# Image 0 of a four-image vision kernel: rows scanned first, and its preparation chained chunk by chunk into the scan

## The chip, the core and the metric

The kernel runs as one program on one core of a Trainium2 chip. The metric is the device time of that core in microseconds (us), from a launch to the last output written. Before the change the median of three runs was 8837.66 us (8813.62 to 8846.13).

## What is computed

The input is a batch of four images, `x` of 4 x 96 x 64 x 64 floats. Three layers follow one another on each image, and the images do not depend on each other.

```python
# layer 0: a selective scan in four directions (k = 0..3), Di = 192 channels, N = 16 states
u      = silu(depthwise_conv3x3(in_proj(norm(x))))
z      = silu(in_proj_z(norm(x)))
delta  = softplus(dt_w[k] @ x_proj[k](u) + dt_b[k])
h      = exp(delta * A) * h + (delta * u) * B          # one step per pixel, 4096 pixels
y_k    = sum_n(h * C) + D * u                          # k=0 rows, 1 columns, 2 and 3 the same backwards
x1     = x + out_proj(norm(y_0 + y_1 + y_2 + y_3) * z)
# layer 1: a deformable 3x3 convolution: offsets from a convolution, then gathers from a table of pixels
# layers 2 and 3: a Fourier mixer, a quantised MLP, a linear attention, a quantised MLP
```

Direction 0 reads an image by rows and direction 2 the same backwards; 1 and 3 read it by columns.

## The kernel before, in words

A Python program writes the instructions of all engines, and keeps its own model of when each engine will be free (`Clock`, line 207). What it writes down is the order on each engine; the chip then runs each engine's list in that order. Three strands are woven together.

The **scan** (`Layer0.scan`, line 816) is the spine. It works through 1536 units: 4 images x 4 directions x 4 steps of 1024 pixels x 24 groups of 8 channels. A unit loads its decays (`fetch`, line 882, on ScalarE's DMA queue), takes their exponential (line 932, ScalarE), spreads its inflow over the states with a matmul (line 938, TensorE), multiplies it with B (line 952, VectorE), runs the recurrence (line 960, VectorE), multiplies with C (line 969, GpSimd) and is summed into a total (line 988, TensorE). The inputs of a unit are fetched from DRAM: B and C once per step (`fetch_step`, line 913), the inflow `du` once per eight units (`fetch_block`, line 920), both on SyncE's queue. Before image 0's first unit is written, `scan` asks for the chunks it needs (`made`, line 835: a chunk is 512 pixels, a step is two chunks). While they are missing it lets the other strands run alone.

The strand **`ends`** (line 1721) prepares images and finishes them: `before(0)`, the constants of layers 2 and 3, `before(1)` to `before(3)`, and then layers 2 and 3 of images 0 to 3, one after the other (`Layers23.image`, line 1688, which first waits until layer 1 of its image is over). The strand **`middle`** (line 1731) writes zeros into the border of the two gather tables (`Layer1.cleared`, line 1125), and then does, image by image, the end of layer 0 (`behind`, line 1010) and layer 1 (`Layer1.image`, line 1139: offsets, positions, and `sample`, line 1284, with one gather per pixel and tap). Beside each unit of the scan the program puts pieces of these two strands where its model finds room. When the scan is over, both strands run to their end.

`before(b)` (line 592) prepares an image in stages, each of which is over before the next begins. `inputs` (615) loads `x`; `normed_rows` (635) normalises it into a padded tile `pad`; `convolved` (672) then loads its weights `wc` and `wz`, and makes the depthwise convolution and the gate `z` for 8 chunks, 18 + 2 matmuls and six loads of an activation table to a chunk, with the results `xa` and `xc` stored to DRAM. After that `before` loads the weights of the projections, and for each chunk makes `projected` (729, both orientations, q = 1 and 0) and six chains of `steps` (751): directions 1, 0+1, 3, 2+3, 0, 2. A chain with two directions holds the last 64 channels of both. A chain is a matmul `pd`, a softplus on ScalarE, VectorE and GpSimd, the store of `de` (delta) to DRAM, a product with u, its split into three bf16 parts by matmuls `pr` and copies, and the store of `du`.

`pipe` (line 273) runs a few such chains side by side: up to `width`, of which a later one may take no step that the earlier ones have not taken `every` + 1 steps before, with three PSUM banks and counted tiles (`ex`, `lw`, `rl`, `du`, `zt`).

SyncE's queue takes its DMAs in order. Where one DMA has to wait for another, or for an engine, all that stand behind it wait as well. Of the eight border writes four go to each table, and they overlap at the corners, so that each waits until the one before it on its table has landed.

Of the kernel before, what the change touches and what calls it, by code (L numbers as in the profile page):

```python
# [272 lines left out]
def pipe(net, chains, width, every=0, **tiles):  # L273
# [5 lines left out]
    while True:  # L279
        if more and len(active) < width:  # L280
            steps = next(chains, None)
            if steps is None:
                more = False
            else:
                active.append(Chain(steps, clock.now()))
                continue
        if not active:
            break
        for n, chain in enumerate(active):
            if chain.new and not net.has_bank():  # L290
                continue
            if any(a.done <= chain.done + every for a in active[:n]):
                continue
            if not all(free[tag] > 0 for tag in chain.takes):
                continue
            if clock.has_room(known.get((chain.kind, chain.done), (1.0,) * 4), chain.ready):
                break
        else:
            yield BLOCKED
            continue  # L300
        for tag in chain.takes:
            free[tag] -= 1
        clock.precede(known.get((chain.kind, chain.done), (0.0,) * 4))
        step = next(chain.steps, None)
        if step is None:
            net.hold(-chain.holds)
            active.remove(chain)
            end = max(end, chain.ready)
            continue
        for tag in step.frees:  # L310
            free[tag] += 1
        known[chain.kind, chain.done] = step.work
        chain.ready = clock.queue(step, chain.ready)
        chain.done += 1
        net.hold(step.holds - chain.holds)
        chain.holds, chain.new, chain.takes = step.holds, step.new, step.takes
        yield None
# [221 lines left out]
class Layer0:  # L539
# [51 lines left out]

    def before(self, b):
        net = self.net
        tc, nc, ins = net.tc, net.nc, net.ins
        with tc.tile_pool(name=f"l0u{b}", bufs=1) as up:
# [3 lines left out]
            with tc.tile_pool(name=f"l0b{b}", bufs=1) as sm:  # L599
# [5 lines left out]
                def chains():  # L605
                    yield self.projected(b, 0, us, xp_a, xp_c, sm, xdbl)
                    for j in range(NCH):
                        for ks in ((1,), (0, 1), (3,), (2, 3), (0,), (2,)):
                            yield self.steps(b, ks, j, us, dtw, sm, xdbl)
                        if j + 1 < NCH:  # L610
                            yield self.projected(b, j + 1, us, xp_a, xp_c, sm, xdbl)
# [3 lines left out]
    def inputs(self, b, up, us):  # L615

        tc, nc, ins = self.net.tc, self.net.nc, self.net.ins
# [4 lines left out]
        nc.sync.dma_start(x, ins["x"][b])  # L622

        def rows(pad, j):
            return pad[:, 1 + j * NR : 1 + (j + 1) * NR, 1 : 1 + W]

        def as_rows(t):
            return t.rearrange("p (h w) -> p h w", w=W)

        with tc.tile_pool(name=f"l0a{b}", bufs=1) as big:  # L630
            pad = big.tile([C, PW, PW], F32, name=f"pad{b}", tag="pad")
            yield from self.normed_rows(b, x, pad, rows, as_rows)
            yield from self.convolved(b, pad, xa, xc, rows, as_rows)

    def normed_rows(self, b, x, pad, rows, as_rows):

        net = self.net
# [34 lines left out]
    def convolved(self, b, pad, xa, xc, rows, as_rows):  # L672

        net = self.net
        tc, nc, ins = net.tc, net.nc, net.ins
        with tc.tile_pool(name=f"l0i{b}", bufs=1) as sm:
            wc = sm.tile([C, 9, 256], F32, name=f"wc{b}", tag="wc")
            nc.sync.dma_start(wc, self.wc_d)
            wz = sm.tile([C, 256], F32, name=f"wz{b}", tag="wz")
            nc.sync.dma_start(wz, ins["w_in"][:, 256:])  # L680
            yield wait(4.0)
            xct_v = xc.rearrange("p (w h) -> p h w", h=H)

            def chain(j):
                cs = slice(j * CH, (j + 1) * CH)
                r0 = j * NR
                for g in range(2):
                    pp = net.mm(f"pc{g}_{b}_{j}")
                    for q in range(9):
                        dy, dx = divmod(q, 3)  # L690
                        nc.tensor.matmul(  # L691
                            pp,
                            lhsT=wc[:, q, g * 128 : (g + 1) * 128],
                            rhs=pad[:, r0 + dy : r0 + dy + NR, dx : dx + W],
                            start=(q == 0),
                            stop=(q == 8),
                        )
                        if q < 8:
                            yield cost(pe=0.8, holds=1)
                    if g == 0:  # L700
                        nc.scalar.activation(xa[:, cs], pp, AF.Silu, bias=net.vec(V_CBA))
                    else:
                        nc.scalar.activation(xc[:64, cs], pp[:64], AF.Silu, bias=net.vec(V_CBC, 64))
                        nc.scalar.activation(
                            xct_v[64:, r0 : r0 + NR, :],
                            as_rows(pp[64:]),
                            AF.Silu,
                            bias=net.vec(V_CBC, 64, 64),
                        )
                    net.exp_and_log()  # L710
                    yield cost(pe=0.8, act=4.0, new=True, takes="zt" if g else "")
                zts = []
                for g, (c0, n) in enumerate(((0, 128), (128, D2))):
                    pz = net.mm(f"pz{g}_{b}_{j}")
                    nc.tensor.matmul(pz, lhsT=wz[:, c0 : c0 + 128], rhs=rows(pad, j), start=True, stop=True)
                    zt = sm.tile([128, CH], F32, name=f"zt{g}_{b}_{j}", tag=f"zt{g}")
                    nc.scalar.activation(zt[:n], pz[:n], AF.Silu)
                    zts.append((c0, n, zt))
                net.exp_and_log()
                yield cost(pe=2.0, act=3.8)  # L720
                for c0, n, zt in zts:
                    nc.sync.dma_start(self.z_d[b][c0 : c0 + n, cs], zt[:n])
                nc.sync.dma_start(self.u_d[b][:128, cs], xa[:, cs])
                nc.sync.dma_start(self.u_d[b][128:, cs], xc[:64, cs])
                yield wait(frees="zt")

            yield from pipe(self.net, (chain(j) for j in range(NCH)), 2, zt=1)

    def projected(self, b, j, us, xp_a, xp_c, sm, xdbl):
# [5 lines left out]
        for q in (1, 0):  # L735
# [9 lines left out]
            yield cost(pe=1.3, act=0.7, new=q == 1)  # L745
        for q in (1, 0):
# [4 lines left out]
    def steps(self, b, ks, j, us, dtw, sm, xdbl):  # L751
# [14 lines left out]
        for k in ks:  # L766
            q = k % 2
            o, m = (pd[64 * q : 64 * q + 64], slice(128, DI)) if both else (pd, slice(0, 128))
            nc.tensor.matmul(o, lhsT=dtw[:, k, m], rhs=xdbl[q, j], start=True, stop=True)  # L769
# [14 lines left out]
        if not both and ks[0] % 2:  # L784
# [31 lines left out]
    def scan(self):  # L816
# [5 lines left out]
            for k in (1, 3, 0, 2)  # L822
# [889 lines left out]
def layers23(net, x2, out):  # L1712
# [4 lines left out]
    with ExitStack() as ctx:  # L1717
# [3 lines left out]
        def ends():  # L1721
            yield from l0.before(0)
# [8 lines left out]
        def middle():  # L1731
            yield from l1.cleared()
# [59 lines left out]
```

## Time and profile before

| What | us |
|---|---|
| median of three runs | 8837.66 |
| the profiled execution's own time | 8879.74 |
| its span, first to last instruction | 8877.9 |
| first recurrence (line 960) starts | 359.4 |
| last recurrence starts | 7667.6 |
| last gather of layer 1 (line 1301) starts | 8350.2 |
| VectorE busy (share of the span) | 6807.1 (77%) |
| TensorE busy | 6652.4 (75%) |
| GpSimd busy | 5620.9 (63%) |
| ScalarE busy | 4943.6 (56%) |

The profiled execution took 42 us more than the median of the runs. The span falls into a head without scan (to 359 us), the scan (to 7670 us) and a tail in which the two strands run out (to 8878 us). Shares of the whole span hide this: what bounds the time has to be read in each of the three.

In the lines shown below a piece of the chain of waits has its start in us, its length in us, and its engine or DMA with the tile written and the tile read; a letter and number such as L691 is a line of the kernel. A row of the table by stretches has the limits in us, and for each engine its busy time with the number of instructions in brackets, then the granted TensorE clock as a share of full speed, the DMA engines' busy share and GB/s.

### The profile page before, as it was taken

Reading aid. Unit: us, or ns where it says so; the run is one execution under the profiler, and the core shown is the slowest. Engines: PE = TensorE matmul, PEld = TensorE weight load, DVE = VectorE, ACT = ScalarE, POOL = GpSimd, SP = SyncE. Lnnn points to the kernel's source line nnn. Section 1 sums busy time; section 2 is a strip of 40 time slices with the busy share of each in tenths; the row PEclk is TensorE's granted clock in tenths of the full one; section 3 lists DMA queues with packets and bytes.
Section 4 is the critical chain, followed back from the end, with each engine's and each line's share of the span. In section 5 each row is a group of like instructions: output and inputs, shape, how many; then the busy total and the mean of one; then the engine's idle time right before and its main releaser. Section 6 shows DMA issues by size and latency. Waiting matters only on the chain.

```text
span 8877.9 us, 96298 instructions
## 1 busy us (share of the span) xinstructions
PE 6652.4 (75%) x31960; PEld 2922.8 (33%) x31960; DVE 6807.1 (77%) x5091; ACT 4943.6 (56%) x9062; POOL 5620.9 (63%) x4307
## 2 busy tenths in 40 slices
PE   6665967687767778777667888776778877787797
PEld 2111311122122224311222455222445532265383
DVE  0488889987888988788898887788878888636514
ACT  3564656555556768745566666445656774423323
POOL 0365656665668888666588888566887886447400
PEclk8786977788778779877777888787888887788797
DMA  1476777767678888876788988676888987444310
GB/s 48 134 201 178 187 186 223 202 176 184 190 204 228 234 225 231 212 181 187 200 226 223 230 223 225 152 181 173 212 228 211 234 204 170 108 128 146 96 55 11
DMA packets 775989, 1608.40 MB, mean 181 GB/s; under 512 B 247809, under 2 KB 339357, under 8 KB 773382
## 3 DMA queue, kind: packets, MB, share of 16 engines
q10 hardware_dynamic: 244224, 843.17, 37.0%
q1 hardware_dynamic: 457542, 532.51, 22.2%
q0 software_dynamic: 73728, 226.57, 9.7%
q8 instruction: 256, 4.19, 0.2%
q14 instruction: 239, 1.96, 0.1%
HBM read 1345.62 MB, written 256.29 MB: 180 GB/s over the span
## 4 chain that ended last, share of the span: by engine, by line
PE 35%; DVE 28%; DMA 16%; ACT 8%; issue 8%; POOL 3%; SPq 2%; ACTq 1%; DVEq 0%; another core or an unknown queue 0%; POOLq 0%
DVE hh L960 14%; DVE db L952 7%; DMA du<-du 6%; PE pc L691 4%; PE py L988 4%; PE f L1428 3%; PE db L938 3%; PE ps L1334 3%; DMA da<-de 2%; ACT g L1313 2%; PE pd L1350 2%; POOL hh L969 1%; ACT da L932 1%; PE h L1469 1%; PE py L983 1%
## 5 line engine op out<-in xcount | busy, mean ns | idle before, releaser
L969 POOL TENSOR_TENSOR hh<-hh,bc 128x1024 f32<-128x1024 f32 x1536 | 3659.8, 2385 | 346.0 <-DVE hh L960 233.6
L960 DVE TENSOR_TENSOR_SCAN hh<-da,st,db 128x1024 f32<-128x1024 f32 x1152 | 2701.0, 2345 | 236.2 <-PE py L988 98.9
L952 DVE TENSOR_TENSOR db<-db,bc 128x1024 f32<-128x1024 f32 x1536 | 1863.3, 1213 | 557.5 <-PE db L938 551.6
L932 ACT ACTIVATE da<-da,w_al 128x1024 f32<-128x1024 f32 x1536 | 1741.8, 1146 | 648.2 <-DMA da<-de 295.3
L938 PE MATMUL db<-du,rep 96*128 96x512 bf16 x3072 | 1105.0, 448 | 810.8 <-DVE hh L960 748.9
L1301 POOL DMA_INDIRECT g<-table,idx x1152 | 1210.6, 1051 | 407.2 <-issue 176.0
L988 PE MATMUL py<-hh,w_fold 128*32 128x512 f32 x6144 | 1055.6, 762 | 26.6 <-POOL hh L969 8.8
L1313 ACT ACTIVATE g<-g,wt 128x96 f32<-128x96 f32 x3456 | 963.9, 364 | 167.6 <-DMA du<-du 52.2
L960 DVE TENSOR_TENSOR_SCAN hh<-da,db 128x1024 f32<-128x1024 f32 x384 | 877.1, 2284 | 68.9 <-PE py L988 22.8
L938 PEld LDWEIGHTS <-rep 96*128 96x128 bf16 x3072 | 284.5, 107 | 1764.0 <-issue 1126.3
L1334 PE MATMUL ps<-w_ident,g 128*96 128x128 f32 x3744 | 675.3, 320 | 215.0 <-ACT g L1313 138.0
L780 POOL TENSOR_TENSOR lw<-lw,w 128x512 f32<-128x512 f32 x192 | 244.2, 1272 | 825.5 <-DVE w L778 815.6
L967 POOL COPY st<-hh 128x1 f32<-128x1 f32 x1152 | 232.4, 202 | 725.3 <-DVE hh L960 682.0
L1334 PEld LDWEIGHTS ps<-w_ident,g 128*96 128x96 f32 x3744 | 480.1, 141 | 569.4 <-ACT g L1313 249.6
L691 PE MATMUL pc<-pad,wc 96*128 96x512 f32 x1152 | 547.8, 615 | 53.4 <-DMA wc<-wc_d 46.3
L1342 ACT COPY st<-ps 96x384 f32<-96x384 f32 x384 | 179.7, 472 | 458.2 <-PE ps L1334 350.6
L801 PE MATMUL pr<-ex,w_ident 128*128 128x512 f32 x384 | 281.0, 822 | 170.0 <-DVE ex L791 87.7
L778 DVE SCALAR_TENSOR_TENSOR w<-w,ex 128x512 f32<-128x512 f32 x192 | 155.1, 808 | 289.8 <-ACT w L775 289.7
L691 PEld LDWEIGHTS pc<-pad,wc 96*128 96x128 f32 x1152 | 216.5, 195 | 336.4 <-issue 305.1
L988 PEld LDWEIGHTS py<-hh,w_fold 128*32 128x32 f32 x6144 | 155.1, 123 | 516.8 <-issue 393.8
L769 PE MATMUL pd<-xd,w_dtw 103*64 103x512 f32 (+1 forms) x512 | 268.0, 802 | 65.8 <-DVE rl L782 26.1
L1350 PE MATMUL pd<-st,wdc 96*128 96x256 f32 x1152 | 302.4, 411 | 7.8 <-ACT st L1342 4.1
(250 smaller groups left out, 8807.7 us busy)
## 6 DMA issues: line engine op xcount, KB each, us to landing
da<-de ACTq DMA_DIRECT2D x1536, 512.0 KB
du<-du SPq DMA_DIRECT2D x512, 192.0 KB
bc<-bcd SPq DMA_DIRECT2D x128, 512.0 KB
du<-du SPq DMA_DIRECT2D x128, 384.0 KB
y<-yb SPq DMA_DIRECT2D x384, 128.0 KB
de<-rl SPq DMA_DIRECT2D x128, 256.0 KB
m<-in_dft SPq DMA_DIRECT2D x128, 256.0 KB
ad<-y ACTq DMA_DIRECT2D x192, 128.0 KB
```

Source lines behind the costliest of these rows:

```text
L691: nc.tensor.matmul(pp, lhsT=wc[:, q, g * 128 : (g + 1) * 128], rhs=pad[:, r0 + dy : r0 + dy + NR, dx : dx + W], start=(q == 0), stop=(q == 8),
L801: nc.tensor.matmul(pr, lhsT=net.ident, rhs=ex, start=True, stop=False)
L932: self.net.nc.scalar.activation(u.da, u.da, AF.Exp, scale=self.al[:, a : a + 1])
L938: self.net.nc.tensor.matmul(db[:, h, :], lhsT=self.rep[:96, u.s % 4, :], rhs=u.du[u.s // 4][:, h * CH : (h + 1) * CH], start=True, stop=True,)
L952: self.net.nc.vector.tensor_mul(u.db, u.db, u.bc[:, 0, :])
L960: nc.vector.tensor_tensor_scan(u.along(u.hh), u.along(u.da), u.along(u.db), first, ALU.mult, ALU.add)
L969: self.net.nc.gpsimd.tensor_mul(u.hh, u.hh, u.bc[:, 1, :])
L988: nc.tensor.matmul(py[p0 : p0 + 32], lhsT=self.fold[:, u.i, :], rhs=hc[:, h * CH : (h + 1) * CH], start=u.sums["add"] is None and u.i == 0 ...
L1301: nc.gpsimd.indirect_dma_start(out=g[:, k, :], out_offset=None, in_=self.tables[b % 2], in_offset=bass.IndirectOffsetOnAxis(ap=idx[:, n : ...
L1313: nc.scalar.activation(pixel, pixel, AF.Identity, scale=wt[:, n, c : c + 1])
L1334: nc.tensor.matmul(pt[:, k, :], lhsT=g[:, k, c * C : (c + 1) * C], rhs=net.ident, is_transpose=True, start=(c == 0), stop=(c == corners - 1),)
L1350: nc.tensor.matmul(po, lhsT=wdc[:, k, :], rhs=st[:, k, :], start=(k == 0), stop=(k == 8))
```

## The change

Image 0 gets a preparation of its own, `first`, in the place of `before(0)`:

- `wc`, `wz` and the weights of the projections are requested right behind `x`, before the normalisation.
- The convolution of chunk j+1, the row projection of chunk j and its three chains of `steps` (directions 0, 0+2, 2) are now in one `pipe` of width 6; the projection of chunk j waits for a token that the convolution of chunk j gives. The `lane` argument lets convolutions be ordered among themselves only, and the other chains among themselves only. The columns (1, 1+3, 3) follow in a second `pipe`.
- The scan of image 0 takes the directions in the order 0, 1, 3, 2 instead of 1, 3, 0, 2.
- A chain 0+2 or 1+3 holds two directions of one orientation. Its product with u, one instruction before, is two instructions of 64 partitions, one of which reads a turned view.
- `middle` waits for the first recurrence before it clears the borders.

Images 1 to 3 are prepared as before.

```diff
-def pipe(net, chains, width, every=0, **tiles):
+def pipe(net, chains, width, every=0, lane=None, **tiles):
...
-            if any(a.done <= chain.done + every for a in active[:n]):
+            if any(
+                a.done <= chain.done + every
+                for a in active[:n]
+                if lane is None or (a.kind is lane) == (chain.kind is lane)
+            ):
                 continue
...
+    def first(self):
...
+        with tc.tile_pool(name=f"l0u{b}", bufs=1) as up, tc.tile_pool(name=f"l0b{b}", bufs=1) as sm:
+            us = []
+            x = self.tokens(b, up, us)
+            xp_a, xp_c = (net.load(q, sm) for q in ("xp_a", "xp_c"))
+            dtw = net.load("dtw", sm)
+            xdbl = {}
+            with tc.tile_pool(name=f"l0a{b}", bufs=1) as big, tc.tile_pool(name=f"l0i{b}", bufs=1) as cp:
+                pad = big.tile([C, PW, PW], F32, name=f"pad{b}", tag="pad")
+                weights = self.conv_weights(b, cp)
+                yield from self.normed_rows(b, x, pad)
+
+                def rows_first():
+                    yield self.conv(b, 0, pad, us, weights, cp)
+                    for j in range(NCH):
+                        if j + 1 < NCH:
+                            yield self.conv(b, j + 1, pad, us, weights, cp)
+                        yield self.projected(b, j, us, xp_a, xp_c, sm, xdbl, (0,), f"c{j}")
+                        for ks in ((0,), (0, 2), (2,)):
+                            yield self.steps(b, ks, j, us, dtw, sm, xdbl)
+
+                tokens = {f"c{j}": 0 for j in range(NCH)}
+                yield from pipe(
+                    net, rows_first(), 6, every=2, lane=Layer0.conv.__code__,
+                    ex=3, lw=1, rl=2, du=2, zt=1, **tokens,
+                )
+
+            def columns():
+                for j in range(NCH):
+                    yield self.projected(b, j, us, xp_a, xp_c, sm, xdbl, (1,))
+                    for ks in ((1,), (1, 3), (3,)):
+                        yield self.steps(b, ks, j, us, dtw, sm, xdbl)
+
+            yield from pipe(net, columns(), 5, every=2, ex=3, lw=1, rl=2, du=2)
...
+    def conv_weights(self, b, sm):
+
+        nc = self.net.nc
+        wc = sm.tile([C, 9, 256], F32, name=f"wc{b}", tag="wc")
+        nc.sync.dma_start(wc, self.wc_d)
+        wz = sm.tile([C, 256], F32, name=f"wz{b}", tag="wz")
+        nc.sync.dma_start(wz, self.net.ins["w_in"][:, 256:])
+        return wc, wz
+
+    def conv(self, b, j, pad, us, weights, sm):
...
-                yield wait(frees="zt")
+        yield wait(frees=f"zt c{j}")
...
+        if both and ks[0] % 2 == ks[1] % 2:
+            q, xc = ks[0] % 2, us[2]
+            own, far = slice(64 * q, 64 * q + 64), slice(64 - 64 * q, 128 - 64 * q)
+            turned = xc.rearrange("p (a b) -> p b a", a=64)
+            nc.vector.tensor_mul(ex[own], rl[own], xc[own, cs])
+            nc.vector.tensor_mul(
+                ex[far].rearrange("p (a b) -> p a b", b=64),
+                rl[far].rearrange("p (a b) -> p a b", b=64),
+                turned[far, j * NR : (j + 1) * NR, :],
+            )
...
-            for k in (1, 3, 0, 2)
+            for k in ((1, 3, 0, 2) if b else (0, 1, 3, 2))
...
-            yield from l0.before(0)
+            yield from l0.first()
...
         def middle():
+            while not l0.scanned[1]:
+                yield BLOCKED
             yield from l1.cleared()
```

The body of `conv` is that of the chain in `convolved`, moved into a method of its own.

## The prediction, on record before the changed kernel ran

> **What bounds the kernel now.** I read the table by stretches first, because the shares of the whole span mix three different stages.
>
> ```profile
> 0.00:357.00 357.00, 215.83 (x450) 84.24 (x451) 38.94 (x69) 155.83 (x193) 14.83 (x19) 0.81 0.23 67
> 357.00:7670.00 7313.00, 5489.00 (x24594) 2183.59 (x24594) 6243.02 (x4241) 4441.81 (x8179) 5229.06 (x3975) 0.80 0.78 202
> 7670.00:8414.00 744.00, 570.52 (x3888) 389.67 (x3888) 397.99 (x565) 208.74 (x420) 373.20 (x312) 0.79 0.42 120
> 8414.00:8878.00 464.00, 377.06 (x3028) 265.33 (x3028) 127.16 (x217) 137.18 (x270) 3.83 (x1) 0.86 0.12 35
> ```
>
> The columns are PE, weight loads, DVE, ACT, POOL. The head does almost no VectorE work (39 us of 357). In the scan VectorE is busy 85%, and 1536 units in 7313 us are 4.76 us each, with little variation: 205 to 217 recurrences start in each 1000 us from 1000 to 7000. The tail is bound by TensorE and by order. Then I read the chain of waits through the head, in two windows:
>
> ```profile
> 16.58 18.85 DMA table<-zero
> 35.45 10.53 DMA table<-zero
> 46.00 10.66 DMA table<-zero
> ...
> 86.14 10.71 DMA table<-zero
> ...
> 97.18 12.23 DMA wc<-wc_d
> ...
> 109.55 2.90 PE pc L691 x3
> ```
>
> ```profile
> 337.55 10.39 DMA du<-du
> ...
> 348.82 12.57 DMA du<-du
> ```
>
> The convolution's weights stand on SyncE's queue behind eight border writes, each of which waits for the one before. TensorE had finished the normalisation's matmuls at 64.9 and starts the convolution at 109.5. The eight chunks then take until 256 (TensorE 141 us busy of 147), the projection weights until 274, two chunks of steps in all directions until 337.5, and the last store and fetch of `du` until 361 (the first recurrence starts at 359.4). Last, the chain in the tail:
>
> ```profile
> 7672.95 7.08 DMA out<-t
> 7680.05 8.68 DMA t<-x
> ```
>
> ```profile
> 8407.33 7.07 DMA out<-t
> 8414.58 8.84 DMA t<-x
> ```
>
> `out<-t` is an image leaving layers 2 and 3, `t<-x` the next one entering. As it happens, image 1 leaves 3 us after the last recurrence. Images 2 and 3 follow one after the other, and that strand sets the end: layer 1 of image 3 (last gather at 8350) is over just before image 2 is. Whatever delays `ends` against the scan is added to the tail.
>
> [...] 201 KB in 10.6 us is 19 GB/s, while `x` (1536 KB from 16.05 to about 27.8) runs at 134. [...] the trace has 1.28 us, six to a chunk of convolution. [...] 1.00 granted from 150 to 250, 0.64 from 300 to 350 among short chains. [...] The turned product (L785) takes 1.02 us alone, near 283 us, and 1.72 in the mean, mostly beside the scan[...].
>
> **Step 1: the head.** The weights are now requested at about 18 us, and the border writes are gone from here. `wc` needs 12.2 us and has 45. So the convolution starts at about 65 instead of 109.5. Of its order on TensorE the changed program tells: ahead of the first spread stand 76 convolution matmuls (4.2 chunks), 8 of the gate, 6 projections, 9 `pd`, and 5 `pr` sets. A float matmul of 512 columns is two passes of 0.43 us at full clock, so (76+8+6+9+5) x 0.86 = 89 us, and 9 bf16 ones of about 0.5 add 4.5; with the first few at half clock 3 more: 97 us. A chain goes TensorE, ScalarE (2.7 us, and a silu between two table loads may be queued in front, 3.3 us), VectorE, GpSimd, VectorE, ScalarE and back. The order leaves about 8 matmuls (7 us) to cover some 9 us, so I charge 3 us for each of 5 chains, 15 us. The needed `du` is finished some 4 us before that point. Store and fetch of `du` were 22 us from 337.5 and stay. First recurrence: 65 + 97 + 15 - 4 + 22 = 195, or **164 us earlier**. Bounds: with no waits 180 (179 earlier); at the clock of 0.64 throughout, 65 + 97 / 0.64 - 4 + 22 = 235 (124 earlier).
>
> **Step 2: the scan.** Four chunks of convolution, with their 16 stores of u and z on SyncE (0.5 us of issue each), move beside it, and four more chains. Does it get longer? I counted the instructions between first and last unit in both orders: VectorE 4239 to 4218, ScalarE 9999 to 9914, GpSimd 3975 to 3958, TensorE 19522 to 19403. Priced with the means of the trace, VectorE has 6398 us before and 6397 after (means of the whole trace, hence not the 6243 of the table; 16 split products are in it, each some 1.0 + 1.7 us where 1.0 stood). The load is unchanged because work has left the other end (step 3). The eight border writes now stand on SyncE between the fetch of the first block and the stores of chunk 3; queued behind them are stores of `de` and `du` and the fetches of blocks 1 and 2. Two chains of four writes hold the queue for 2 x 3 x 10.6 = 64 us and 14 units last 14 x 4.76 = 67 us, so most of it hides and I charge 10 (bounds 0 and 60). Against that, the row chains that step 2 and 3 need now stand at units 37 and 53, not 43 and 67, for the same deadlines 48 and 72; before, the fetch of `du` stood 11.8 us in the chain at 541 and again at 587. I give back 10. Net **0**, bounds -75 and +75 (1%: the windows above spread more, and the order of the whole scan is dealt anew).
>
> **Step 3: the tail.** The order also tells where `ends` stands. Image 1's preparation begins at unit 129 instead of 90, image 2's at 325 (285), image 3's at 674 (601), image 0's linear attention ends at 1269 (1179). At the last unit image 1 is no longer finished: all of its 32 key-value products and its second MLP (40 chunks instead of 32 are left) remain, on VectorE 876 instructions instead of 783. The same stretch of image 3, alone, lasts from the second half of its normalisation at 8761 to the last addition at 8870: 109 us. While layer 1 of image 3 runs, `ends` goes at 0.63 of its pace alone (of image 2's 464 us, 427 in the 682 us from 7688 to 8370), but that supply is already used, so the excess is paid in full. One more pair of gated chunks in `behind(3)` makes `middle` perhaps 15 us later, which costs 15 x 0.37 = 6. **115 us later**; bounds 70 and 160.
>
> **The sum.** 8877.9 - 164 + 0 + 115 = 8829, 49 us less than the span of before. The profiled execution (8879.7) lies 42 above the median; the difference is taken from the median: 8837.7 - 49 = **8789**. About 0.5% is what a measurement of this kernel can tell from no change, so this lies at its edge. Most of what the head gives is given back in the tail, since the work taken out of the head displaces `ends`.
>
> **The rivals.**
> - *The head's gain survives.* The tail is as before, because image 1's rest is hidden beside layer 1 of image 3, whose window has VectorE busy only 365 us of 682: 8838 - 164 = 8674. Against it: TensorE is busy 546 of 682 there.
> - *The head shrinks less.* Chains and convolution wait for each other on TensorE and ScalarE, the clock stays at 0.64: 8838 - 124 + 115 = 8829. For it: three banks, and 11 us of ScalarE per convolution chunk ahead of each chain's copies.
> - *The border writes starve the scan: slower.* On SyncE each holds back `du`. Two in flight together took 18.6 us (from 56.99). Uncovered, all eight at that price are 149 us: 8789 + 149 = 8938. From 49 us uncovered the gain is gone, from 93 it is slower by 0.5%. Against it: only what exceeds the units' own time counts.
>
> That the change doesn't start the scan earlier is excluded by the order: 63 VectorE instructions ahead of it, not 71, and only half the convolution.
>
> **Chances.** Forecast 0.50 (its own range 8720 to 8870, of which 0.29 below 8793), head's gain kept 0.16, head shrinks less 0.20, starved 0.14. So faster by over 0.5%: 0.29 + 0.16 = 0.45; slower: 0.14; the rest, 0.41, within. The bounds of the steps, combined as independent (-15/+40, 75, 45), are about 92 on either side; with the rivals' ends 8690 to 8890.
>
> **What would show it.** First recurrence near 195 in the trace, `pc` from about 65, no `table<-zero` before the scan; recurrences at 21 per 100 us from there, 24 of them within 135 us; last recurrence near 7510; image 1 leaving 109 to 170 us after it, not 3. Wrong if the scan's length moves by over 75 us, or if the tail stays at 1208 us.

## The result, and the profile after

The changed kernel takes 8782.35 us (median of 8 runs, 8754.13 to 8796.72) against 8836.12 us for the kernel before beside it (8 runs, 8804.81 to 8868.07). The ratio is 0.9941, with a 95% interval of 0.9924 to 0.9959: 0.6% faster. The forecast was 8789.

The profiled execution of the changed kernel has a span of 8794.9 us (own time 8796.72, 14 above its median; the one of before lay 44 above its median here). The table by stretches, cut at its own events, shows where the time went. Columns are as before: limits, length, PE, weight loads, DVE, ACT, POOL, granted clock, DMA share, GB/s.

```profile
0.00:200.00 200.00, 130.55 (x274) 51.58 (x275) 34.37 (x63) 97.98 (x127) 9.04 (x15) 0.88 0.31 87
200.00:366.00 166.00, 105.02 (x306) 34.64 (x306) 107.99 (x76) 83.40 (x104) 72.58 (x56) 0.78 0.51 148
366.00:7491.00 7125.00, 5317.31 (x24137) 2135.66 (x24138) 6142.70 (x4143) 4339.35 (x7997) 5141.39 (x3900) 0.81 0.78 205
7491.00:7716.00 225.00, 170.44 (x612) 66.70 (x610) 75.19 (x139) 81.53 (x167) 38.96 (x36) 0.81 0.28 62
7716.00:8309.00 593.00, 491.06 (x3604) 357.71 (x3604) 375.32 (x521) 178.40 (x366) 337.20 (x285) 0.85 0.43 127
8309.00:8795.00 486.00, 392.03 (x3028) 276.03 (x3028) 127.03 (x217) 137.25 (x270) 3.83 (x1) 0.82 0.12 37
```

The first row is the head, 200 us instead of 359. The next two are the scan; its first 24 units, up to the first recurrence that carries a state on, are a row of their own. The last three are the tail: 225 us until image 1 leaves, where before it left 3 us after the last recurrence, then the stretches of images 2 and 3. The second row is the odd one: VectorE is busy 65% of it, in the next one 86%. In the kernel before, the same 24 units took 133 us, and VectorE was busy 85% of them:

```profile
359.00:492.00 133.00, 89.78 (x245) 25.00 (x244) 113.22 (x93) 87.29 (x130) 79.80 (x62) 0.80 0.65 184
```

This is the chain of waits in the head, where the border writes and the gap ahead of the convolution stood before:

```profile
55.91 8.63 PE lnb L516 x16
64.54 20.62 PE pc L750 x48
...
177.80 3.28 DMA du<-du
181.10 22.54 DMA du<-du
```

The convolution (`pc`) now follows on the last matmuls of the normalisation (`lnb`). The chain in the tail:

```profile
7715.55 8.35 DMA out<-t
7723.92 11.49 DMA t<-x
```

Here and below, "head" runs to the start of the first recurrence, "scan" from there to the end of the last (2.35 us after it starts), "tail" from there to the end of the span.

| profiled execution | head | scan | first 24 units of it | tail | span | image 1 leaves, after the scan's end |
|---|---|---|---|---|---|---|
| before | 359.4 | 7310.6 | 132.8 | 1207.9 | 8877.9 | 3 |
| changed | 199.6 | 7291.6 | 166.3 | 1303.6 | 8794.9 | 224 |
| difference | -159.8 | -19.0 | +33.5 | +95.7 | -83.0 | +221 |

The spans differ by 83 us and the medians by 54; the other 29 are only that the profiled execution of before lay further above its median (43.6 us against 14.4). So the differences of scan and tail in this table are no surer than some 30 us, and the last section shows that the tail of one program varied by more.

### The profile page after: what moved, and what is told of

Read it like the earlier page. It is cut to its first block, busy times and chain, and to the rows that moved or that the text cites. A ratio compares the mean times of both kernels' runs of the same rounds, so it can differ in the third digit from the quotient of the medians.

```text
span 8794.9 us, 96335 instructions
## 1 busy us (share of the span) xinstructions
PE 6606.4 (75%) x31960; PEld 2922.3 (33%) x31960; DVE 6862.6 (78%) x5155; ACT 4917.9 (56%) x9030; POOL 5603.0 (64%) x4291
## 4 chain that ended last, share of the span: by engine, by line
PE 34%; DVE 27%; DMA 17%; ACT 8%; issue 7%; POOL 2%; SPq 2%; ACTq 1%; DVEq 0%; POOLq 0%
DVE hh L1028 13%; DVE db L1020 7%; DMA du<-du 4%; PE pc L750 4%; PE py L1056 4%; PE f L1496 3%; PE ps L1402 3%; DMA da<-de 3%; PE db L1006 3%; ACT g L1381 2%; DMA bc<-bcd 2%; PE pd L1418 2%; ACT da L1000 2%; PE h L1537 1%; POOL hh L1037 1%
## 5 line engine op out<-in xcount | busy, mean ns | idle before, releaser
L1402 PE MATMUL ps<-w_ident,g 128*96 128x128 f32 x3744 | 694.4, 328 | 195.8 <-ACT g L1381 130.5
L750 PE MATMUL pc<-pad,wc 96*128 96x512 f32 x1152 | 570.7, 629 | 12.2 <-DVE rl L840 3.7
L827 PE MATMUL pd<-xd,w_dtw 103*64 103x512 f32 (+1 forms) x512 | 249.1, 740 | 53.6 <-DVE rl L840 28.4
L1505 ACT COPY d<-f 128x512 f32<-128x512 f32 x192 | 111.8, 583 | 305.3 <-PE f L1496 291.2
```

The costliest lines, as they stand in the source:

```text
L750: nc.tensor.matmul(pp, lhsT=wc[:, q, g * 128 : (g + 1) * 128], rhs=pad[:, r0 + dy : r0 + dy + NR, dx : dx + W], start=(q == 0), stop=(q == 8),
L1402: nc.tensor.matmul(pt[:, k, :], lhsT=g[:, k, c * C : (c + 1) * C], rhs=net.ident, is_transpose=True, start=(c == 0), stop=(c == corners - 1),)
```

## The experiments

There were three sets of four kernels, each set on another chip. The kernel before was run beside each, with medians of 8886.4, 8897.0 and 8826.6 us, so times are compared within a set, and ratios to the kernel before (with their 95% intervals) across sets. The expected times of the first set were worked out from 8837 and 8782 us; since its kernel before took 50 us more, they are to be read as differences.

Where "the order" is named, it is the order of VectorE's instructions as each program writes it; it is known without a run. Two marks in it tell where the strand `ends` stands: the unit of the scan beside which image 0's linear attention ends (before: 1179; changed: 1269), and the number of VectorE instructions after the last recurrence (783; 876).

**1. Weights early alone.** The changed kernel's loads, with the stages, the chains and the order of directions of before; the border writes stand at the start again, behind the loads.

```diff
-                def rows_first():
...
                 yield from pipe(
...
+                    net, (self.conv(b, j, pad, us, weights, cp) for j in range(NCH)), 2,
+                    zt=1, **{f"c{j}": 0 for j in range(NCH)},
                 )
...
+            def chains():
...
+                    for ks in ((1,), (0, 1), (3,), (2, 3), (0,), (2,)):
                         yield self.steps(b, ks, j, us, dtw, sm, xdbl)
...
-            for k in ((1, 3, 0, 2) if b else (0, 1, 3, 2))
+            for k in (1, 3, 0, 2)
...
-            while not l0.scanned[1]:
-                yield BLOCKED
             yield from l1.cleared()
```

> Only the early weights: image 0 keeps the stages and the order of directions of the kernel before, but its convolution and projection weights are requested right behind x, ahead of the border writes, which stay at the start. My theory (only the waiting in the head is a gain; work that is moved out of the head comes back in the tail): the head loses 45 us of wait for wc and about 15 for the projection weights, first recurrence near 300, the tail stays near 1208, so about 60 less, a median near 8776, as fast as the whole change. Rival (the gain comes from starting the scan 160 us earlier, whatever fills the head): a median near 8836 - 0.35 x 60 = 8815, since this starts it only 60 earlier.

Measured: 8855.09 us, ratio 0.9954 (0.9935 to 0.9973). Head 312.1, scan 7297.6, tail 1221.4. The order of VectorE is that of the kernel before, and the profile keeps the head's 47 us (scan -13, tail +13); the medians differ by 8886 - 8855 = 31. The theory's gain of 60 was about twice too large; the rival's 21 was nearer. Still, this part of the change alone is worth most of what the whole is.

**2. The border first.** The changed kernel without the wait in `middle`, so that the border writes are issued at the start, behind the weights.

```diff
         def middle():
-            while not l0.scanned[1]:
-                yield BLOCKED
             yield from l1.cleared()
```

> The changed kernel with the border writes back at the start, where they now stand behind the weights: middle no longer waits for the first recurrence. My theory: the first 24 units, which took 166 us instead of 133, lose the border writes from SyncE's queue and come back to about 135, so 30 us less, a median near 8752; first recurrence unchanged near 200. Rival (the slow first units come from the convolution on TensorE and from chunk 3 being late, and the border writes are hidden): first 24 units stay at 155 to 166, a median within 10 us of 8782.

Measured: 8824.19 us, ratio 0.9923 (0.9898 to 0.9948). The first 24 units take 131.2 us instead of 166.3, with the order unchanged; the head grows to 215.3. So the slow start of the scan belongs to the border writes, not to the convolution that now runs beside it. Against the changed kernel the ratios give some 16 us (0.9941, first set of runs) or 28 us (0.9955, experiment 5), where 30 were expected; the intervals overlap.

**3. The pipeline alone.** The changed kernel with the border writes back at the start, and with the weights requested where they stood before, behind the normalisation and those writes.

```diff
-            xp_a, xp_c = (net.load(q, sm) for q in ("xp_a", "xp_c"))
-            dtw = net.load("dtw", sm)
...
+                yield from self.normed_rows(b, x, pad)
                 weights = self.conv_weights(b, cp)
-                yield from self.normed_rows(b, x, pad)
+                xp_a, xp_c = (net.load(q, sm) for q in ("xp_a", "xp_c"))
+                dtw = net.load("dtw", sm)
+                yield wait(4.0)
...
         def middle():
-            while not l0.scanned[1]:
-                yield BLOCKED
             yield from l1.cleared()
```

> The pipeline alone: rows first and chunk by chunk as in the changed kernel, but all weights are requested after the normalisation, behind the border writes at the start, as before. My theory: convolution from about 110, first recurrence near 245, 115 earlier than before, but the tail is as long as in the changed kernel (about 1300), so only 20 less than before, a median near 8816. Rival (an earlier start is what gains): 115 / 160 of the whole gain, a median near 8797.

Measured: 8883.69 us, ratio 0.9989 (0.9976 to 1.0001): no gain that can be told. The head is 243.3 us, 116 shorter, and it comes back as +111 in the tail (1319.2) and +18 in the scan (7328.6). The theory had expected 20 us of gain. Image 1 leaves 110 us after the scan's end here, against 220 in experiment 2 of the same set, whose tail is 1364: 110 us less of delay are only 45 us less of tail.

**4. Rows first, but staged.** Weights early, border first, all eight chunks of the convolution ahead of the scan as in experiment 1. What differs from that experiment is that the chains are split, all rows and then all columns, and that image 0 is scanned in the directions 0, 1, 3, 2 to match. The edit is shown against the changed kernel.

```diff
-                def rows_first():
...
                 yield from pipe(
...
+                    net, (self.conv(b, j, pad, us, weights, cp) for j in range(NCH)), 2,
+                    zt=1, **{f"c{j}": 0 for j in range(NCH)},
                 )
 
-            def columns():
+            def oriented(q):
                 for j in range(NCH):
...
+                    yield self.projected(b, j, us, xp_a, xp_c, sm, xdbl, (q,))
+                    for ks in ((q,), (q, q + 2), (q + 2,)):
                         yield self.steps(b, ks, j, us, dtw, sm, xdbl)
...
+            for q in range(2):
+                yield from pipe(net, oriented(q), 5, every=2, ex=3, lw=1, rl=2, du=2)
...
         def middle():
-            while not l0.scanned[1]:
-                yield BLOCKED
             yield from l1.cleared()
```

> Rows first, but in stages: weights early and border writes at the start, all eight chunks convolved before the first projection, then rows, then columns. My theory: convolution from 65 to 212, two chunks of three chains instead of six, first recurrence near 265, 95 earlier than before, of which 35 is work moved behind the start and comes back in the tail (about 1245), so about 60 less, a median near 8776. Rival (starting earlier is what gains, at 54 of 160 us): a median near 8804.

Measured: 8936.69 us, ratio 1.0054 (1.0040 to 1.0067). This was a plain miss: a gain was expected and it is slower. The head is 294.7, where 265 was expected, and the scan 7266.0. Both are shorter than in experiment 1, but the tail is 1359.7 instead of 1221.4, and image 1 leaves 232 us after the scan. No convolution has moved beside the scan here, and yet the order has `ends` where the changed kernel has it: unit 1255, 877 instructions after the last recurrence. In the order, 38 chains of image 0 stand beside 72 units in the kernel before, 42 beside 98 here and 42 beside 110 in the changed kernel. So the give-back does not come, or not mainly, from the convolution. With the chains split, the planner places them more slowly (some 2.3 units to a chain instead of 1.9), and all that `ends` does later lies later.

**5. The changed kernel again,** as a base for the second set.

> The changed kernel once more, so that it stands beside the next three on one chip. Theory: the split is the kernel's own: first recurrence near 200 us, first 24 units of the scan near 166 us, tail (end of the last recurrence to the end of the span) near 1304 us, ratio to the kernel before 0.994. Rival: a part of the tail belongs to the chip, since the runs of the other chip all show tails of 1320 to 1364 us where rows and columns are split: then the tail is near 1360 here and the ratio above 0.996.

Measured: 8850.48 us, ratio 0.9955 (0.9939 to 0.9970). Head 201.1, first 24 units 163.6, scan 7301.4: as on record. The tail is 1378.9, 75 longer than in the first profile, for the same program; the last section comes back to it. The ratio agrees with the first one, so the rival fell in that, though not on the tail.

**6. One MLP less in the tail.** Image 1's second MLP is left out, so that its output lacks that layer.

```diff
-            yield from self.ffn3.run(b, t)
+            if b != 1:
+                yield from self.ffn3.run(b, t)
```

> The changed kernel with image 1's second MLP left out (that image's output lacks it). Theory, the step of the prediction: what image 1 has left when the scan ends lies ahead of everything else in the tail, so the tail falls by what that MLP takes alone, 57 us in the kernel before for image 3's (8813 to 8870 us), and image 1 leaves some 60 to 160 us after the last recurrence instead of 224; median -50 to -70 us against the changed kernel beside it. Rival: layer 1 of image 3 sets the tail, image 1's work lies beside it: image 1 leaves earlier, the last gather starts and the span ends as before, median within 15 us of the changed kernel.

Measured: 8819.02 us, ratio 0.9910 (0.9886 to 0.9935), 31 us less than experiment 5. Image 1 leaves 122 us after the scan's end instead of 219, 97 earlier, and the tail falls by 56 (1322.6), as the theory had it; but the scan is 15 longer, and the medians lie between theory and rival. So what image 1 has left does count in the tail, but not one for one: the MLP, which alone takes 57 us, takes 97 beside layer 1 of image 3, and 56 of those return.

**7 and 8. More background per unit.** The planner gives each unit of the scan an allowance of time, the constant `PACE` (line 204), by which the background's due time advances. It is 4.5 us, a unit takes 4.76. Experiment 7 raises it in the kernel of experiment 2, experiment 8 in the kernel before.

```diff
-PACE = 4.5
+PACE = 4.75
```

> The changed kernel with the border of the table first, and the planner's allowance of background work for one unit of the scan raised from 4.5 to 4.75 us, nearly the 4.76 us that a unit takes. By the order of its instructions image 1's work is all placed within the scan (VectorE instructions after the last recurrence: 726 instead of 876). Theory: the lag of the background behind the scan is what the tail pays, and VectorE, 85% busy in the scan, has room for it: tail down from about 1360 to 1150-1210 us, scan up by 0 to 100 us, ratio to the kernel before 0.977 to 0.987. Rival: the scan pays for what the tail gives, since each of the 150 instructions moved costs its 0.66 us there and waits with it: ratio 0.990 to 0.995, as with the old allowance.

> The kernel before with the same allowance of 4.75 us alone. By the order of its instructions the VectorE instructions after the last recurrence fall from 783 to 726, as many as with the changed kernel. Theory: the changed kernel's head is given back only because the background lags more under 4.5 us; with 4.75 us neither kernel has image 1 in the tail, so this one gains less (tail -40 to -110 us, ratio 0.988 to 0.996), and the changed kernel with the same allowance is then ahead of this one by most of its head, 100 us or more. Rival: the give-back is in the rest of the tail; then the two kernels with 4.75 us stand as far apart as with 4.5, 50 to 70 us.

Measured: 8791.64 us, ratio 0.9897 (0.9875 to 0.9919), and 8909.59 us, ratio 1.0028 (1.0013 to 1.0043). Both have 726 VectorE instructions after the last recurrence, and their tails are 1125.6 and 1132.9 us, practically the same; their scans grow to 7445.8 and 7428.1. Experiment 8's tail is as the theory said, its ratio is not: the scan paid 117 us. Experiment 7 fell at the rival's edge for the same reason. What matters is their distance, and there the theory held: 118 us, against 62 for the same kernel under the old allowance (experiment 2 against the kernel before). Once `ends` lags in neither kernel, 118 of the head's 142 us (214.3 against 356.6) survive.

**9. The border late alone.** Experiment 1, with the wait in `middle` back.

```diff
         def middle():
+            while not l0.scanned[1]:
+                yield BLOCKED
             yield from l1.cleared()
```

> The kernel before with the weights early, as in the first of these runs, and the border of the table written only once image 0's scan has begun: two of the change's three parts, without the pipeline of rows. Theory: the border on SP beside the first units is a loss of its own, whatever the order of the work: first recurrence 0 to 15 us earlier than the 312 us of weights early alone, first 24 units 20 to 35 us longer than its 135, ratio 0.996 to 0.999 against 0.9954 there. Rival: the loss seen in the changed kernel comes from its conv beside the scan, not from the border: first 24 units stay at 130 to 138 us and the ratio is 0.993 to 0.996.

Measured: 8819.94 us, ratio 0.9992 (0.9973 to 1.0010). The head is 22 us shorter than in experiment 1 (289.8), the first 24 units 41 longer (176.0 against 135.0), both somewhat more than expected. With the old order of work the late border costs the first units at least as much, so it is a loss of its own.

**10. The border spread.** The changed kernel, with each border write of 67 rows split into one of 64 and one of 3.

```diff
-                    nc.sync.dma_start(v[lo : lo + 2].rearrange("y x d -> x y d"), zero)
-                    yield wait(6.0)
-                    nc.sync.dma_start(v[:, lo : lo + 2], zero)
-                    yield wait(6.0)
+                    for edge in (v[lo : lo + 2].rearrange("y x d -> x y d"), v[:, lo : lo + 2]):
+                        for a, z in ((0, 64), (64, GW)):
+                            nc.sync.dma_start(edge[a:z], zero[: z - a])
+                        yield wait(6.0)
```

> The changed kernel with each of the eight writes of the border split in two, 64 rows and 3 rows[...]. Theory: the first 24 units wait for du behind a border write[...], so with the writes spread they fall from 164 to 125-140 us while the first recurrence stays near 200; median -15 to -35 us against the changed kernel (ratio 0.9955 on this chip): 0.992 to 0.994. Rival: what delays the first units is the issue order on SP[...]: the border's 16 issues now hold SP as long or longer, first 24 units 155 to 180 us, ratio 0.995 to 0.997.

Measured: 8743.46 us, ratio 0.9914 (0.9887 to 0.9941). Head 199.8, first 24 units 132.2, both as the theory said; the ratio is a little better than its 0.992 to 0.994. Against the changed kernel's two ratios, 0.9941 and 0.9955, that is some 24 or 36 us, though the intervals overlap. The waits of SyncE's queue in that stretch (us in total, times, longest) show why. First the changed kernel, then this one:

```profile
SPq L862 <- DVE rl L840: 42.0, 4, 17.5
SPq L1204 <- DMA table<-zero: 19.1, 2, 11.8
SPq L1202 <- DMA table<-zero: 16.7, 2, 8.8
SPq L783 <- DMA table<-zero: 8.8, 1, 8.8
...
SPq L807 <- DMA table<-zero: 1.9, 1, 1.9
```

```profile
SPq L862 <- DVE rl L840: 57.5, 7, 22.7
...
SPq L1204 <- DMA table<-zero: 1.5, 2, 1.3
...
SPq L807 <- DMA table<-zero: 1.0, 1, 1.0
```

In the changed kernel the queue stands still for 19.1 + 16.7 + 8.8 + 1.9 = 46.5 us of these 166 until a border write has landed; with the rows spread it is 2.5 us, although there are twice as many writes to issue. In the kernel before, where the border writes of 67 rows were alone in flight (76 to 97 us), one took 10.6 us for its 201 KB, and the busy share of the DMA engines was 0.06, at 20 GB/s. Why the split writes are waited for less was not shown. What stands behind in that queue is what the scan lives on. The chain of waits has it, first in the changed kernel and then in this one:

```profile
222.17 17.22 DMA du<-du
...
272.51 20.55 issue
...
307.71 19.82 issue
```

```profile
270.47 2.79 issue
...
287.87 6.71 issue
```

The two long stalls ("issue": the engine named next, GpSimd, waited for nothing that the profile shows) shrink to 3 and 7 us, and the fetch of `du` at 222 is gone from the chain. What the first stall waited for shows in the engines' waits of the changed kernel: until 283.7 ScalarE stood idle for a fetch of `du`, and VectorE behind it until 290.7. With the rows spread ScalarE has no such wait. What the second stall waited for was not taken apart.

```profile
ACT da L1000 <- DMA du<-du: 22.5, 1, 22.5
```

**11 and 12. The border spread, with 4.75 and with 4.6 us.** `PACE` as in experiment 7, on the kernel of experiment 10.

> The same with the allowance of 4.75 us a unit. Theory: the two effects add, since one lies in the first 24 units and the other in the balance of scan and tail: head near 200, tail near 1126 and scan near 7440 as with 4.75 us and the border first (ratio 0.9897), 10 us less for the head: ratio 0.987 to 0.990. Rival: the border costs the scan elsewhere once more background runs beside it: ratio 0.990 to 0.993.

> The same with an allowance of 4.6 us: VectorE instructions after the last recurrence 788, between the 876 of 4.5 and the 726 of 4.75. Theory: what a moved instruction costs the scan is the same for the first as for the last (scan +191 us for 150 instructions between 4.5 and 4.75, 1.27 us each), while the tail falls most with image 1's last work: scan near 7370, tail 1210 to 1250, ratio 0.988 to 0.993, not better than 4.75. Rival: the first instructions fit idle time and cost the scan little, the last ones cost it most: scan near 7300, tail as said, ratio 0.984 to 0.988, better than 4.75.

Measured: with 4.75, 8779.33 us, ratio 0.9956 (0.9941 to 0.9972); with 4.6, 8686.91 us, ratio 0.9847 (0.9822 to 0.9871), the fastest kernel of the study, 140 us below the one before. Both theories fell; the rival of experiment 12, a scan near 7300 and a ratio of 0.984 to 0.988, came about. The effects don't add at 4.75: the scan is 7474.7 us, 29 longer than in experiment 7, and the ratio misses both expectations. And the cost of a moved instruction is not constant: from 4.5 to 4.6 the scan pays 18 us (7264.2 to 7282.2) for 74 in the tail (1276.6 to 1202.3); from 4.6 to 4.75 it pays 192 for 98. The table by stretches of the kernel with 4.6:

```profile
197.00:327.00 130.00, 101.83 (x306) 33.96 (x305) 107.15 (x75) 82.62 (x103) 72.38 (x56) 0.86 0.66 188
327.00:7479.00 7152.00, 5443.64 (x24422) 2181.42 (x24422) 6163.72 (x4184) 4392.01 (x8104) 5162.05 (x3913) 0.82 0.78 204
7479.00:7512.00 33.00, 20.34 (x50) 4.89 (x50) 17.51 (x9) 23.02 (x41) 21.19 (x16) 0.55 0.14 38
7512.00:8185.00 673.00, 548.00 (x3851) 387.65 (x3850) 372.93 (x521) 197.08 (x400) 353.27 (x307) 0.84 0.45 128
```

Image 1 leaves 33 us after the scan's end, not 224; 285 more TensorE instructions lie in the scan than in that of the changed kernel (24422 against 24137), in almost the same length, 7152 against 7125 us, the first 24 units aside in both.

Why 4.75 costs so much, the waits of VectorE between 1500 and 7000 us tell in part. With 4.6, then with 4.75:

```profile
DVE db L1020 <- PE db L1006: 404.6, 214, 17.4
DVE hh L1028 <- PE py L1056: 75.2, 78, 5.2
```

```profile
DVE db L1020 <- PE db L1006: 488.5, 230, 14.0
DVE hh L1028 <- PE py L1056: 98.4, 75, 9.7
```

In these 5500 us 1155 recurrences run with 4.6 and 1124 with 4.75. With 4.75 VectorE is less busy (4575 against 4655 us), and in these two lines it waits 107 us longer for the spread and the summing of the units on TensorE. So the loss is not VectorE's time for the moved work, as had been thought: the units wait for TensorE. That engine's busy time is the same (4233 us with 4.6, 4216 with 4.75), so it should be the order in its list, with other work in front of the units' matmuls; that is argued, and which placements do it was not taken apart.

## Why the prediction was right, point by point

The head gave 4 us less than forecast, scan and tail came out 19 us shorter each, and 83 us between the spans is not the 49 of the forecast. That the forecast of the median came within 7 us owes much to the scatter of the two profiled executions, which takes 29 of the 83 away again: the nearness is luck, the direction is not.

**Step 1, the head: right.** First recurrence 199.6 instead of 195. The convolution starts at 64.5 (forecast 65). From there to the store of `du` at 177.8 are 113 us, where the step had 97 + 15 - 4 = 108. In the 97, 3 us stood for a start at half clock, which did not come: the granted clock was 1.00 from 64.5 to 75, where the kernel before had 0.50 from 109.5 to 113, after 44.6 us without a matmul. From 64.5 to 178 it was 0.88 in the mean. The store and fetch end 22 us later, as charged.

**Step 2, the scan: the sum right, one term mis-sized.** The whole scan moved by -19 us, within the bounds of 75. The border was charged 10 us within bounds of 0 and 60. It costs 34: 166.3 us instead of 132.8 for the first 24 units, which were said to stay within 135, and experiments 2 and 10 bring them back to 131 and 132. "Most of it hides" was the weak sentence: the queue was held for 46.5 us, less than the 64 assumed, but most of that was paid. The rest of the scan is 52 us shorter; that is the dealing anew of an order, and no experiment isolates it. That the two offset each other was luck within stated bounds.

**Step 3, the tail: the size right, the working not.** Forecast +115, measured +96; in experiment 5 the same program had a tail 75 us longer, so the agreement could as well have been poorer. Two errors offset each other. Image 1 leaves 224 us after the scan, not 109 to 170: its work goes slower beside layer 1 of image 3 than alone, by 57/97 = 0.59 in experiment 6, near the 0.63 of the prediction, which used that factor for the supply and not for the rest; 109/0.63 would have been 173, and 224 is more still. And "the excess is paid in full" fails: 221 us more of delay are 96 of tail, in experiment 6 97 us less are 56, and between experiments 2 and 3 110 us less are 45. Layer 1 of image 3 goes on meanwhile, so that less should be left afterwards. In keeping with this, TensorE has, in the stretch in which image 2 finishes, 3604 instructions instead of the 3888 of before.

**The reason given for the give-back was too simple.** The prediction had it that the work taken out of the head displaces `ends`. Experiment 4 shows the full give-back with all of the convolution still in the head, and experiment 12 shows the same moved work with hardly any: head 197.0, scan 7282.2 (7310.6 before), tail 1202.3 (1207.9 before). There `ends` stands nearly where it stood before the change (788 instructions after the last recurrence, 783 before), and 140 us are gained, not far from the 164 of the rival "the head's gain survives". Its reason is another, though: image 1's rest isn't hidden in the tail, it is done in the scan. And 4.6 us was not tried in the kernel before, so how much of the 140 it would have gained without the change is open; with 4.75 that kernel gained nothing (experiment 8). What took the gain was an order that lets `ends` lag. In that order, image 0's chains stretch over 110 units instead of 72, and the split, with its order of directions, brings 26 of these 38 more (98 in experiment 4). With 4.6 us they still stretch over 110 in the trace; `ends` makes up the lag later. Image 0's linear attention ends there beside unit 1217, against 1186 before and 1284 in the changed kernel (by the traces, which show it some units later than the order has it). At this allowance the scan had room for the work.

**The other rivals.** "The head shrinks less" is out by the 199.6. "The border writes starve the scan" had the right mechanism and place; at 34 us it stayed below the 49 from which it would have eaten the gain. On the kernel with weights early alone it ate it: experiment 9 against 1, 0.9992 against 0.9954, though these come from two sets and the intervals just touch.

## What to carry to other kernels

A head that is shortened under a planner is worth what the planner's other strands don't lose: compare, in the two orders, where each strand stands at the end of the spine, and if one has fallen back, look first for the constant that rations it (here, with the border spread, 4.5 to 4.6 us a unit was worth as much as the change itself, and 4.75 gave it away again). A DMA queue that works in order, as SyncE's does here, charges every wait to all that stands behind it (46.5 us of waits, 34 of them paid), so small transfers that wait for one another don't become free by being moved beside busy work; splitting each of them (64 rows and 3 instead of 67) brought the waits to 2.5 us and the first 24 units to 132. Parts of one change should be run one at a time: here one was worth 0.5% (the early weights), one nothing as long as it made `ends` lag (the pipeline), and one cost 0.2 to 0.4% (the late border).

## What the runs showed of the hardware that was not expected

The same program had two tails. Between the leaving of images 1 and 2 the changed kernel took 593 us in its first profile and 674 in experiment 5. The row of the first stands in the table of the result (from 7716 to 8309); this is the row of the second, cut 5 us late:

```profile
7721.00:8400.00 679.00, 528.53 (x3604) 377.46 (x3604) 375.29 (x522) 178.51 (x366) 331.84 (x286) 0.81 0.38 113
```

VectorE and ScalarE have the same busy time; TensorE, with 3604 instructions in both, is busy 37 us longer at a granted clock of 0.81 instead of 0.85, and the rest of the 80 us is waiting. The cause stays open. But the other experiments with those 3604 instructions in this stretch point to the set (each ran on one chip) rather than to the single execution: 597 us in experiment 10 (granted clock 0.85 from 7500 to 8000 us, 0.88 from 8000 to 8500), 675 at 0.79 in experiment 2 and 658 at 0.83 in experiment 4. The two short stretches come from where the kernel before took 8836 and 8827 us, the three long ones from where it took 8886 and 8897. No set has two profiles of one program, so this is a pattern of five profiles and not a proof. It is a warning against reading a tail's length across sets; differences of tails above that are small beside 75 us are safe only within one.
